# A convolution block and a two-layer state-space block on one core: preparation steps at other places, a smaller share of C on GpSimd, and byte-wise waits of later pools

## The chip, the core and the metric

The program runs on one core of a Trainium2 chip. The time is the device time of one execution, in microseconds; 18147.85 us is the median of three runs. A core has TensorE (PE, matrix products into PSUM), VectorE (DVE), ScalarE (ACT), GpSimd (POOL), and SyncE (SP), whose queue issues most of the transfers. Each engine takes its instructions strictly in the order of its own queue, and waits at an instruction until what it needs is there.

## The reference

Two layers follow one another on x of 32 images, 96 channels, 56 x 56 points, all in float32. Layer 0 is an inverted bottleneck with a depthwise 3 x 3 convolution and a squeeze-and-excite gate; the change doesn't touch it. Layer 1 runs a state-space block (two layers of it) along the 3136 points of each image, then a 1 x 1 fusion and a batch normalisation over everything:

```
h = layernorm(seq);  xs, z = split(h @ in_w)
xc = silu(causal_conv4(xs) + conv_b)
dt, Bm, Cm = split(xc @ xproj_w)            # 6, 16 and 16 columns
delta = softplus(dt @ dt_w + dt_b)
state[t] = exp(delta[t] * A) * state[t-1] + delta[t] * Bm[t] * xc[t]   # 192 x 16 states
y = sum over the 16 of state * Cm + Dp * xc
seq = seq + (y * silu(z)) @ out_w           # twice, then:
out = batchnorm(fus_w @ [seq, relu(gp(mean x))]) + x
```

## The kernel before, in words

**Units and slots.** The change lies in layer 1. A unit is one of the two state-space layers on 784 tokens of one image (four such pieces, LC = 784, make an image): 128 pieces x 2 = 256 units. A unit has 24 slots (`NT`): 192 channels in three groups `k` of 64, 16 states in four groups `j` of 4, two halves `p` of 32 channels. One slot handles 32 channels x 4 states = 128 partitions of 784 tokens.

**What a slot does.** `decay` (L1004, ScalarE) makes exp(delta * A) into `da`, a PSUM tile of which there are two. `inject` (L1041, GpSimd, one for two slots, four slots ahead) makes `bx` = (delta x) * B. `scan` (L1052, VectorE) runs the recurrence over the 784 tokens. The result times C is split by token: the first `LP` tokens by `product` (L1060, VectorE, for two slots at once), for which `bring` (L1029, ScalarE) copies C's first `LP` tokens into PSUM as `cp`, and the remaining tokens by `rest` (L1068, GpSimd). `reduce` (L1099, PE), four slots later, sums the four states into `y`; `gated` (L1110, VectorE) multiplies the finished `y` of a group by silu(z); `seed` (L1086, ScalarE) starts the next group's `y`.

**The first state group goes another way.** For `j` = 0 (slots 0, 1, 8, 9, 16 and 17) it is `fill` (L1018, 32 small matmuls on PE, two records each) that makes (delta x) * B, into a tile of the same two PSUM buffers (`bp`), from delta x transposed (`ut`) and a diagonal matrix of B. There the decay goes to SBUF (`bx` in the profile's rows of L1004). Delta x is transposed by `turn_u(k)` (L848, PE) into a bank and copied by `keep_u(k)` (L854 and L855, ScalarE); B by `turn_b` (L822, PE) and `diagonal` (L831, L832, ScalarE), from where `scatter` writes it to the diagonal of a zeroed DRAM tile `bdiag`, and `fetch` reads it as `diag`.

**Preparation.** While the scans of one unit run, later units are prepared: `center` (L702, PE) and `square` (L707, ScalarE) twice, `variance` (L712, PE), `root` (L719 to L723, ScalarE: add epsilon, log, exp of -1/2, and the three columns that precede the piece), `newton` (L729 to L734, VectorE, three operations that refine the root), `turn` and `normalise` (L744 PE, L751 ScalarE), `turn_back` and `normal` (L757, L761), the causal convolution as four shifted products (L773), `gate` (L789), a block of SiLU with its two table loads (L677, L678), `project_bc` and `store_bc` (L798 PE, L802 ScalarE), `turn_b`, `project_dt` (L810), a block of softplus. All of their products use the two banks of the pool `l1p`; a product waits until the bank that it is given has been read. Before, `root` leaves its result `rs` in columns 16 to 22 of the bank of `var`, where `newton` reads it.

**The order** is written out by hand. Each step has a time in slots, counted in its own unit; its whole part names the slot (modulo 24 for the running unit), its fraction the place in the slot. Steps with a fraction below 0.05 come first in the slot, ahead of the decays of the slot; then come the decays, `bring`, `scan`, `gated`, `product` of the slot before, `rest`, `fill`, the steps from 0.05 to 0.08, `reduce`, and the remaining steps in order of fraction. So `keep_u(1)` at 54.2 stands at the end of slot 6 on ScalarE, `root` at -7.9 at the end of slot 16, `newton` at -6.3 to -6.1 at the end of slot 17, `square` 1 at -9.99 at the start of slot 14.

**Pools.** A pool opened where an earlier one has been closed waits, at its first use, for everything in the memory under it.

Of the kernel before, what the change touches and what calls it, by code (L numbers as in the profile page):

```python
# [11 lines left out]
F32 = mybir.dt.float32  # L12
# [12 lines left out]
NL, NS, DIN, RANK, KC = 2, 16, 192, 6, 4  # L25
LC = 784
HB = LC // 2
LP = 416
NQ = L // LC
RB = HB // W  # L30
DG = 8
# [29 lines left out]
def conv_mamba_kernel(ctx, tc, a, out):  # L61
# [43 lines left out]
    with ExitStack() as ph:  # L105
# [12 lines left out]
        def loadw(name, shape):  # L118
            t = wts.tile(list(shape), F32, name=name, tag=name)
            sp.dma_start(t, a[name])  # L120
            return t
# [406 lines left out]


    with ExitStack() as ph:  # L530
        wts = ph.enter_context(tc.tile_pool(name="l1w", bufs=1))
        dpool = ph.enter_context(tc.tile_pool(name="l1da", bufs=2, space=PSUM))
        cpool = ph.enter_context(tc.tile_pool(name="l1c", bufs=1, space=PSUM))
        ypool = ph.enter_context(tc.tile_pool(name="l1y", bufs=1, space=PSUM))
        pp = ph.enter_context(tc.tile_pool(name="l1p", bufs=2, space=PSUM))
        udram = ph.enter_context(tc.tile_pool(name="l1u", bufs=3, space=DRAM))
        init = ExitStack()
        once = init.enter_context(tc.tile_pool(name="l1i", bufs=1))

        def loadw(name, shape, pool=wts, by=sp):  # L540
            t = pool.tile(list(shape), F32, name=name, tag=name)
            by.dma_start(t, a[name])
            return t
# [27 lines left out]
        outw = wts.tile([128, NL, NB, C], F32, name="outw", tag="outwb")  # L571
        dp = wts.tile([128, NL, NB, 2], F32, name="dp", tag="dpb")
        for to, k, h, src, hc in pieces():
            sp.dma_start(outw[to, :, k, :], a["outw"][src, :, hc, :])
            s.dma_start(dp[to, :, k, :], a["dp"][src, :, hc, KC + 1 : KC + 3])

        araw = loadw("acol", [128, NL, NT], once, s)
        pick = once.tile([128, NS, 2 * DB - DG], F32, name="pick", tag="pick")
        v.memset(pick, 0.0)
        v.tensor_copy(pick[:, :, DB - DG : DB], eye.rearrange("p (s d) -> p s d", s=NS))  # L580
# [48 lines left out]
        for to, k, h, src, hc in pieces():  # L629
            sp.dma_start(wbc[to, :, k, : 2 * NS], a["xpw"][src, :, hc, RANK:])  # L630
            s.dma_start(wbc[to, :, k, 2 * NS : 2 * NS + RANK], a["xpw"][src, :, hc, :RANK])
        for h in range(2):
            for i in range(NL):
                to = wd[h * 64 + 2 * NS : h * 64 + 2 * NS + RANK, i, :, :]
                s.dma_start(to, a["dtw"][:, i, :].rearrange("r (k m) -> r k m", k=NB))
# [13 lines left out]

        xn = wts.tile([C + 1, KC - 1 + LC], F32, name="xn", tag="xn")  # L650
        g.memset(xn[C : C + 1, :], 1.0)
        none = once.tile([TB, TR + 2], F32, name="none", tag="none")
        v.memset(none, 0.0)
        zdram = ph.enter_context(tc.tile_pool(name="l1z", bufs=1, space=DRAM))
        bdiag = [zdram.tile([TB * (TR + 2)], F32, name=f"bdiag{i}", tag=f"bdiag{i}") for i in range(2)]
        for t in bdiag:
            sp.dma_start(t.rearrange("(p r) -> p r", p=TB), none)
        tails = [wts.tile([C + 1, KC - 1], F32, name=f"tail{i}", tag=f"tail{i}") for i in range(NL)]

        init.close()  # L660
        work = ph.enter_context(tc.tile_pool(name="l1", bufs=1))
        MAIN = "natural_log_exp_and_others"
        nch = B * NQ
        TURNS = (range(NK - NK // 2), range(NK - NK // 2, NK))
# [20 lines left out]
        def prepare(n):  # L685
# [14 lines left out]
            def center(h):  # L700
                ps = d["cen", h] = bank(f"cen_{n}_{h}")
                pe.matmul(ps[:C, :HB], cen, seqs[c, i][:, cols(h)], start=True, stop=True)  # L702

            def square(h):
                if h == 0:
                    d["sq"] = wt([128, LC], "sx", 1, n)[:C]
                s.activation(d["sq"][:, cols(h)], d["cen", h][:C, :HB], AF.Square)  # L707
# [7 lines left out]
            def root():  # L715

                va = d["va"] = wt([TK, NK], "va", 1, n)
                rs = d["rs"] = d["var"][:TK, 16 : 16 + NK]
                s.activation(va, d["var"][:TK, :NK], AF.Identity, bias=epsc[:TK])  # L719
                s.activation(rs, va, AF.Ln)  # L720
                s.activation(rs, rs, AF.Exp, scale=-0.5)
                if q > 0:
                    s.copy(xn[:, : KC - 1], tails[i])  # L723
# [121 lines left out]
            def turn_u(k):  # L845
                ps = d["utp", k] = bank(f"ut_{n}_{k}")
                for b in range(4):
                    pe.transpose(ps[: TSZ[b], b * 128 : b * 128 + 128], d["us"][:, k, TOFF[b] : TOFF[b] + TSZ[b]], eye)  # L848
# [17 lines left out]

            steps = [(-20.5, load)]
            for h in range(2):
                steps += [((-11.9, -10.94)[h], lambda h=h: center(h)), ((-10.98, -9.99)[h], lambda h=h: square(h))]
            steps += [(-9.94, variance), (-7.9, root), *[(t, lambda m=m: newton(m)) for m, t in enumerate((-6.3, -6.2, -6.1))]]  # L870
            for m in range(2):
                steps += [((-6.7, -5.5)[m], lambda m=m: turn(m)), (-5.7 + m, lambda m=m: normalise(m))]
                steps += [(-4.5 + m, lambda m=m: turn_back(m)), (-3.9 + m, lambda m=m: normal(m))]
# [4 lines left out]
            for k in range(NB):  # L878
                steps += [(t, lambda k=k, o=o: conv(k, o)) for o, t in taps[k]]
                steps += [((3.1, 5.1, 6.1)[k], lambda k=k: keep("xc", 3, "xs", k))]  # L880
                steps += [((11.06, 11.07, 12.06)[k], lambda k=k: gate(k)), ((12.01, 12.02, 13.01)[k], lambda k=k: keep("z", 3, "zp", k))]
            steps += [(17.6, project_bc), (18.2, store_bc), (18.6, turn_b), (19.2, diagonal)]
            for k in range(NB):
                steps += [((20.6, 21.5, 21.6)[k], lambda k=k: project_dt(k)), ((21.2, 22.1, 22.2)[k], lambda k=k: keep("dl", 1, "dtp", k))]
                steps += [((43.5, 53.6, 56.06)[k], lambda k=k: turn_u(k)), ((44.1, 54.2, 57.01)[k], lambda k=k: keep_u(k))]
            for m in range(6):
                steps += [(26.9 + m, lambda m=m: scatter(*divmod(m, 3)))]
            steps += [(32.1, lambda: spread("delta", d["dl"], slice(0, NB)))]
# [244 lines left out]
        with tc.manual_schedule():  # L1133
            for at in range(min(todo), max(todo) + 1):
                for m in (2, 3):
                    if 0 <= at + m < total and by_pe(at + m) and (at + m) % 2 == 0 and ahead(at + m)[0] == m:
                        lend(at + m)
                if 0 <= at + 4 < total:
                    inject(at + 4)
                for u, step in todo.get(at, ()):  # L1140
                    if u < 0.05:
                        step()
                if 0 <= at - LAG < total:
                    seed(at - LAG)
                if 0 <= at + 1 < total and not by_pe(at + 1):
                    decay(at + 1)
                for x in range(at, at + 5):
                    pair = x // 2 * 2
                    if 0 <= x < total and by_pe(x) and pair - ahead(pair)[x - pair] == at:
                        decay(x)  # L1150
                if 0 <= at < total:
                    bring(at)
                for step in early.get(at, ()):
                    step()
                if 0 <= at < total:
                    scan(at)
                if 0 <= at - LAG - 1 < total:
                    gated(at - LAG - 1)
                if 0 <= at - 1 < total:
                    product(at - 1)  # L1160
                if 0 <= at - 2 < total:
                    save(at - 2)
                if 0 <= at < total:
                    rest(at)
                if 0 <= at + 1 < total and by_pe(at + 1):
                    fill(at + 1)
                for u, step in todo.get(at, ()):
                    if 0.05 <= u < 0.08:
                        step()
                if 0 <= at - LAG < total:  # L1170
                    reduce(at - LAG)
                for u, step in todo.get(at, ()):
                    if u >= 0.08:
                        step()
                for t, tag in BEFORE[at % NT]:
                    fetch(at + t, (tag,))


    with ExitStack() as ph:
        last = ph.enter_context(tc.tile_pool(name="last", bufs=6))  # L1180
        one = ph.enter_context(tc.tile_pool(name="last1", bufs=1))
        mv = one.tile([C, 2], F32, name="mv", tag="mv")
        off = one.tile([C, 1], F32, name="off", tag="off")
        v.tensor_reduce(mv, stats, AX.X, ALU.add)
        v.tensor_scalar(mv, mv, 1.0 / (B * L), None, ALU.mult)
        v.tensor_add(off, mv[:, 0:1], pivot)
        v.tensor_mul(off, off, off)
        v.tensor_sub(mv[:, 1:2], mv[:, 1:2], off)
        inv, sh = bn_fold(one, cp[:, BNG : BNG + 1], cp[:, BNB : BNB + 1], mv[:, 0:1], mv[:, 1:2], C, 1, "bn")
        for b in range(B):  # L1190
            pre = last.tile([C, L], F32, name=f"lp{b}", tag="lp")
            sp.dma_start(pre, pred[b])
            s.activation(pre, pre, AF.Identity, bias=sh, scale=inv)
            g.dma_start(out[b], pre, accum_op=ALU.add, max_dma_last_dim=4 * L // 2)
# [61 lines left out]
```

## Time and profile before

| What | us |
|---|---|
| median of 3 runs (18144.67 to 18149.34) | 18147.85 |
| the profiled execution: its own time | 18136.26 |
| its span (18134.5), layer 0 until | 2901.9 |
| setup of layer 1 and preparation of the first units, until the first scan at | 3023.2 |
| 256 units, until the end of the last scan at | 17836.6 |
| last stage (batch normalisation, residual), until | 18134.5 |

The prediction shows lines of four views. The page's first lines give each engine's busy time, its share of the span and its instructions. A line of the page's groups gives line, engine, operation, what is written from what, the shape, the count, then busy time in us and the mean of one in ns, then the idle time of the engine just ahead of such instructions and what ended most of it. A line of the waits gives engine and line, what it waited for, the total in us, how many times, and the longest. A line of the timeline gives the start in us, the duration, engine, line, operation and shapes, and in brackets the idle time before it and what ended it. The granted clock of PE was 0.919 of full speed on average over the execution: it falls to half for stretches of 3.4 or 6.8 us, at other places in each unit.

### The profile page before, as it was taken

What the parts mean: (1) busy time and instruction counts of PE and PEld (TensorE: products, weight loads), DVE (VectorE), ACT (ScalarE), POOL (GpSimd) and SP (SyncE); (2) the same over time, 40 slices, a digit from 0 to 9 for tenths busy, and PEclk for the clock granted to TensorE, in tenths of its full rate; (3) what the DMA queues carried; (4) which work ended last, traced back from release to release, by engine and by line L of the source; (5) the groups of instructions that cost most, each with busy time, mean ns of one, the idle gap of its engine ahead of it and who ended that gap; (6) DMA issues with size and microseconds to landing.
All of it is one profiled execution on the core that took longest, in us unless ns stands there. A gap on an engine that the chain in (4) does not pass through costs nothing.

```text
span 18134.5 us, 515855 instructions
## 1 busy us (share of the span) xinstructions
PE 15647.2 (86%) x212542; PEld 8205.4 (45%) x212542; DVE 16799.6 (93%) x12755; ACT 14155.9 (78%) x26476; POOL 14150.6 (78%) x6254
## 2 busy tenths in 40 slices
PE   9999998888888888888888888888888888888882
PEld 4444444444444444444444444444444444444441
DVE  9999996999999999999999999999999999999993
ACT  5555555888888888888888888888888888888884
POOL 0000003999999999999999999999999999999993
PEclk9999998999999999999999999999999999999995
DMA  1111113777777777777777777777777777777778
GB/s 35 29 29 29 29 29 93 186 184 187 182 185 182 184 187 184 183 184 183 184 186 184 183 183 182 185 187 184 184 183 183 184 186 184 183 183 183 185 184 219
DMA packets 1723535, 2893.15 MB, mean 160 GB/s; under 512 B 712886, under 2 KB 950670, under 8 KB 1714790
## 3 DMA queue, kind: packets, MB, share of 16 engines
q1 hardware_dynamic: 1712534, 2821.54, 60.4%
q0 software_dynamic: 6656, 38.54, 1.0%
q8 instruction: 1668, 27.33, 0.7%
q14 instruction: 693, 5.68, 0.1%
q10 hardware_dynamic: 1984, 0.07, 0.0%
HBM read 2402.42 MB, written 455.82 MB: 158 GB/s over the span
## 4 chain that ended last, share of the span: by engine, by line
PE 25%; ACT 19%; issue 11%; DMA 10%; DVE 8%; SPq 6%; POOL 4%; ACTq 0%; POOLq 0%; DVEq 0%
PE bp L1018 8%; DVE hh L1052 5%; ACT da L1004 5%; PE y L1099 4%; SPq L982 3%; ACT bx L1004 3%; DVE hc L1060 3%; PE bc L798 3%; PE z L789 3%; DMA deltab<-deltad 3%; PE o L909 2%; DMA bdiag<-bt 2%; SPq L969 2%; POOL hc L1068 2%; POOL bx L1041 2%
## 5 line engine op out<-in xcount | busy, mean ns | idle before, releaser
L1041 POOL TENSOR_TENSOR bx<-ub,B 128x1568 f32<-128x1568 f32 x2304 | 8172.1, 3547 | 16.3 <-DMA diag<-bdiag 13.2
L1052 DVE TENSOR_TENSOR_SCAN hh<-da,state,bx 128x784 f32<-128x784 f32 x3456 | 6273.7, 1838 | 144.8 <-ACT da L1004 133.3
L1068 POOL TENSOR_TENSOR hc<-hh,C 128x736 f32<-128x736 f32 x3072 | 5416.3, 1763 | 714.3 <-DVE hh L1052 398.1
L1004 ACT ACTIVATE da<-deltab,acol 128x784 f32<-128x784 f32 x4608 | 4249.3, 922 | 916.0 <-DVE hh L1052 914.0
L1018 PE MATMUL bp<-diag,ut 91*32 91x91 f32 (+1 forms) x98304 | 3005.8, 280 | 436.3 <-ACT ut L854 351.4
L1099 PE MATMUL y<-hc,rel 128*32 128x392 f32 x24576 | 2911.8, 546 | 522.1 <-ACT y L1086 517.8
L1018 PEld LDWEIGHTS bp<-diag,ut 91*32 91x32 f32 (+1 forms) x98304 | 2652.1, 123 | 1285.3 <-DVE hh L1052 524.1
L1060 DVE TENSOR_TENSOR hc<-hh,cp 128x832 f32<-128x832 f32 x3072 | 3071.8, 1000 | 0.1
L1052 DVE TENSOR_TENSOR_SCAN hh<-bx,state,bp 128x784 f32<-128x784 f32 x1152 | 2117.4, 1838 | 297.8 <-PE bp L1018 269.9
masks.py:197 POOL MEMSET eye<- 128x128 f32 x2 | 0.4, 205 | 2892.6 <-ACT x L427 2892.3
L773 PE MATMUL xs<-xn,wx 97*64 97x392 f32 x12288 | 2240.2, 507 | 0.4 <-ACT xc L784 0.4
L1052 DVE TENSOR_TENSOR_SCAN hh<-da,bx 128x784 f32<-128x784 f32 x1152 | 2025.2, 1778 | 70.6 <-ACT da L1004 65.5
L340 DVE SCALAR_TENSOR_TENSOR h<-hpad,hp,h 128x1568 f32<-128x1568 f32 x1024 | 1895.5, 1851 | 33.2
L1029 ACT COPY cp<-C 128x416 f32<-128x416 f32 x3072 | 1570.4, 511 | 10.3 <-DVE hc L1060 8.8
L1004 ACT ACTIVATE bx<-deltab,acol 128x784 f32<-128x784 f32 x1536 | 1463.4, 953 | 0.0
L773 PEld LDWEIGHTS xs<-xn,wx 97*64 97x64 f32 x12288 | 817.9, 137 | 1366.7 <-issue 1271.0
L1099 PEld LDWEIGHTS y<-hc,rel 128*32 128x32 f32 x24576 | 609.2, 115 | 1521.2 <-ACT y L1086 983.6
L307 PE MATMUL dw<-hpad,diag 32*32 32x392 f32 x36864 | 1111.3, 518 | 0.1
L798 PE MATMUL bc<-xc,wbc 64*64 64x392 f32 x3072 | 634.6, 547 | 318.8 <-DVE rs L734 295.0
L245 PE MATMUL c<-x,w 96*128 96x392 f32 x2048 | 774.2, 520 | 117.8 <-ACT hpad L252 95.8
L864 POOL TENSOR_TENSOR us<-dl,xc 128x392 f32<-128x392 f32 x768 | 788.2, 1026 | 90.4 <-ACT dl L677 90.4
L1052 DVE TENSOR_TENSOR_SCAN hh<-bx,bp 128x784 f32<-128x784 f32 x384 | 682.9, 1779 | 174.3 <-PE bp L1018 138.4
(195 smaller groups left out, 20108.1 us busy)
## 6 DMA issues: line engine op xcount, KB each, us to landing
ub<-ud SPq DMA_DIRECT2D x3072, 196.0 KB
deltab<-deltad SPq DMA_DIRECT2D x3072, 196.0 KB
C<-bcd SPq DMA_DIRECT2D x4096, 98.0 KB
diag<-bdiag SPq DMA_DIRECT2D x1024, 294.8 KB
B<-bcd SPq DMA_DIRECT2D x3072, 98.0 KB
deltad<-dl SPq DMA_DIRECT2D x512, 294.0 KB
ud<-us SPq DMA_DIRECT2D x1536, 98.0 KB
x<-in_x_dram SPq DMA_DIRECT2D x32, 1176.0 KB
```

The lines of the kernel that those rows point to most:

```text
L307: pe.matmul(ps[r][to : to + 32, :HB], diag[src, n, t, :], hb[src, r0 : r0 + RB, dx : dx + W], start=t == 0, stop=t == 8, skip_group_check= ...
L340: v.scalar_tensor_tensor(acc, src, tap, acc, ALU.mult, ALU.add)
L773: pe.matmul(d["xs", k][h * 64 : h * 64 + 64, :HB], wx[:, i, o, k * 64 : k * 64 + 64], xn[:, o + h * HB : o + h * HB + HB], start=o == 0, s ...
L798: pe.matmul(ps[r, :HB], wbc[r, i, k], d["xc"][r, k, :], start=k == 0, stop=k == NB - 1)
L1004: s.activation(das[at], d["delta", k][:, p, :], AF.Exp, scale=acol[:, j, i, 2 * k + p : 2 * k + p + 1])
L1018: pe.matmul(ps[sg * DB : sg * DB + DB, o : o + z], d["ut", k][:z, b, h, p * DB : p * DB + DB], dg[:z, sg // 2, h, x : x + z, sg % 2], star ...
L1029: s.copy(cps[at], data[n]["C", j][:, :LP])
L1041: g.tensor_mul(bx, data[n]["u", k], beside(data[n]["B", j]))
L1052: v.tensor_tensor_scan(hhs[at - p][:, p, :], das.pop(at), bxs.pop(at), state[i][:, t : t + 1] if c % NQ else 0.0, ALU.mult, ALU.add,)
L1060: v.tensor_mul(hcs[at - 1][:, :, :LP], hhs[at - 1][:, :, :LP], beside(cps.pop(at)))
L1068: g.tensor_mul(hcs[at - 1][:, :, LP:], hhs[at - 1][:, :, LP:], beside(data[n]["C", j][:, LP:]))
L1099: pe.matmul(yps[k][r0 : r0 + DB, :HB], rel, hc[:, p, h * HB : h * HB + HB], start=False, stop=j == SG - 1, skip_group_check=True,)
```

## The change

- **Delta x copies.** `keep_u(1)` moves from 54.2 to 54.04, and a new loop, after the decay of the slot and ahead of the decays of the first state group, takes the steps with fractions from 0.03 to 0.05.
- **Squares.** The second `center` moves from -10.94 to -10.97, the second `square` from -9.99 to -10.96, into the new loop of slot 13.
- **Root.** `root` moves from -7.9 to -6.9 (end of slot 17), `newton` from -6.3, -6.2, -6.1 to -5.95, -5.9, -5.85 (slot 18, behind `product`). Its result is a tile `ra` in SBUF instead of columns of the bank of `var`.
- **B's transposes.** `turn_b` moves from 18.6 to 19.15, behind the `reduce` of slot 19.
- **C.** `LP` becomes 424: VectorE and ScalarE take 424 tokens of C, GpSimd 360 instead of 368.
- **Pools.** The later pools get `reuse_waits="tile"`: a tile waits for what lay in its own bytes. The zeros for `bdiag` become a tile of the work pool, set by GpSimd and written from ScalarE's queue; five weight loads of SP and one of ScalarE go to GpSimd's queue, and eight of SP to ScalarE's.

```diff
-LP = 416
+LP = 424
...
-        wts = ph.enter_context(tc.tile_pool(name="l1w", bufs=1))
+        wts = ph.enter_context(tc.tile_pool(name="l1w", bufs=1, reuse_waits="tile"))
...
-        def loadw(name, shape, pool=wts, by=sp):
+        def loadw(name, shape, pool=wts, by=g):
...
-            sp.dma_start(outw[to, :, k, :], a["outw"][src, :, hc, :])
             s.dma_start(dp[to, :, k, :], a["dp"][src, :, hc, KC + 1 : KC + 3])
-        araw = loadw("acol", [128, NL, NT], once, s)
+        araw = loadw("acol", [128, NL, NT], once)
...
             s.dma_start(wbc[to, :, k, 2 * NS : 2 * NS + RANK], a["xpw"][src, :, hc, :RANK])
+            s.dma_start(outw[to, :, k, :], a["outw"][src, :, hc, :])
...
-        none = once.tile([TB, TR + 2], F32, name="none", tag="none")
-        v.memset(none, 0.0)
...
+        init.close()
+        work = ph.enter_context(tc.tile_pool(name="l1", bufs=1, reuse_waits="tile"))
+        none = work.tile([TB, TR], F32, name="none", tag="diag", bufs=1)
+        g.memset(none, 0.0)
         for t in bdiag:
-            sp.dma_start(t.rearrange("(p r) -> p r", p=TB), none)
+            s.dma_start(t[: TB * TR].rearrange("(p r) -> p r", p=TB), none)
-        init.close()
-        work = ph.enter_context(tc.tile_pool(name="l1", bufs=1))
...
-                rs = d["rs"] = d["var"][:TK, 16 : 16 + NK]
+                rs = d["rs"] = wt([TK, NK], "ra", 1, n)
...
-                steps += [((-11.9, -10.94)[h], lambda h=h: center(h)), ((-10.98, -9.99)[h], lambda h=h: square(h))]
-            steps += [(-9.94, variance), (-7.9, root), *[(t, lambda m=m: newton(m)) for m, t in enumerate((-6.3, -6.2, -6.1))]]
+                steps += [((-11.9, -10.97)[h], lambda h=h: center(h)), ((-10.98, -10.96)[h], lambda h=h: square(h))]
+            steps += [(-9.94, variance), (-6.9, root), *[(t, lambda m=m: newton(m)) for m, t in enumerate((-5.95, -5.9, -5.85))]]
...
-            steps += [(17.6, project_bc), (18.2, store_bc), (18.6, turn_b), (19.2, diagonal)]
+            steps += [(17.6, project_bc), (18.2, store_bc), (19.15, turn_b), (19.2, diagonal)]
...
-                steps += [((43.5, 53.6, 56.06)[k], lambda k=k: turn_u(k)), ((44.1, 54.2, 57.01)[k], lambda k=k: keep_u(k))]
+                steps += [((43.5, 53.6, 56.06)[k], lambda k=k: turn_u(k)), ((44.1, 54.04, 57.01)[k], lambda k=k: keep_u(k))]
...
                 for u, step in todo.get(at, ()):
-                    if u < 0.05:
+                    if u < 0.03:
                         step()
                 if 0 <= at - LAG < total:
                     seed(at - LAG)
                 if 0 <= at + 1 < total and not by_pe(at + 1):
                     decay(at + 1)
+                for u, step in todo.get(at, ()):
+                    if 0.03 <= u < 0.05:
+                        step()
```

## The prediction

> **What bounds the kernel now.** I read the page's busy shares first, then its groups, then the table of waits, then one unit of work in the timeline, engine by engine.
>
> ```profile
> span 18134.5 us, 515855 instructions
> PE 15647.2 (86%) x212542; PEld 8205.4 (45%) x212542; DVE 16799.6 (93%) x12755; ACT 14155.9 (78%) x26476; POOL 14150.6 (78%) x6254
> L1041 POOL TENSOR_TENSOR bx<-ub,B 128x1568 f32<-128x1568 f32 x2304 | 8172.1, 3547 | 16.3 <-DMA diag<-bdiag 13.2
> L1052 DVE TENSOR_TENSOR_SCAN hh<-da,state,bx 128x784 f32<-128x784 f32 x3456 | 6273.7, 1838 | 144.8 <-ACT da L1004 133.3
> L1068 POOL TENSOR_TENSOR hc<-hh,C 128x736 f32<-128x736 f32 x3072 | 5416.3, 1763 | 714.3 <-DVE hh L1052 398.1
> L1060 DVE TENSOR_TENSOR hc<-hh,cp 128x832 f32<-128x832 f32 x3072 | 3071.8, 1000 | 0.1
> ```
>
> The four scan groups hold 6144 scans, 24 to a unit, so 256 units. The timeline has the first scan at 3023.2 us and the end of the last at 17836.6: 57.87 us a unit. VectorE stands still before scans for 144.8 + 297.8 + 70.6 + 174.3 = 687.5 us, 2.69 a unit, and is busy otherwise. GpSimd's groups sum to (8172.1 + 5416.3 + 788.2) / 256 = 56.2 us a unit, so GpSimd is within 2 us of being the bound, and its own idle time is mostly waiting for scans. What can be won is VectorE's 2.69 us. The waits say where it goes (columns: total us, times, longest):
>
> ```profile
> DVE hh L1052 <- PE bp L1018: 408.3, 535, 1.7
> POOL hc L1068 <- DVE hh L1052: 398.1, 199, 5.6
> ACT bcs L802 <- PE bc L798: 382.5, 255, 4.9
> PE bp L1018 <- ACT ut L854: 351.4, 256, 1.6
> PE bc L798 <- DVE rs L734: 295.0, 233, 2.7
> DVE hh L1052 <- ACT da L1004: 198.8, 487, 1.2
> ```
>
> 1.59 us a unit is a scan that waits for the 64 matmul records of `fill`, which wait in their turn 1.37 us a unit for ScalarE's copy `ut`. Slots 6 to 8 of the unit at 15229.7 show it:
>
> ```profile
> 15243.89 0.91 ACT L1004 ACTIVATE da<-deltab,acol 128x784 f32<-128x784 f32 x1
> 15244.73 0.94 ACT L1004 ACTIVATE bx<-deltab,acol 128x784 f32<-128x784 f32 x1
> 15245.57 0.47 ACT L784 COPY xc<-xs 128x392 f32<-128x392 f32 x1
> 15245.94 0.26 ACT L854 COPY ut<-ut 120x128 f32<-120x128 f32 x1
> ...
> 15244.04 0.65 PE L848 MATMUL ut<-eye,us 128*120 128x128 f32 x4 [0.20 <-ACT xc L784]
> 15246.25 2.61 PE L1018 MATMUL bp<-diag,ut 120*32 120x120 f32 x64 [1.56 <-ACT ut L854]
> ...
> 15248.99 1.85 DVE L1052 TENSOR_TENSOR_SCAN hh<-bx,state,bp 128x784 f32<-128x784 f32 x1 [1.05 <-PE bp L1018]
> ```
>
> The transposes are done at 15244.69, but ScalarE takes a decay (`bx`) and a copy (`xc`) before it copies them.
>
> **Delta x copies, and what limits the gain.** `keep_u(1)` moves ahead of those two: its first half starts at 15244.73 instead of 15245.94, 1.21 us sooner. Nothing is added; the later `bx` and `xc` have slots to spare. `fill(8)` also needs the buffer of scan 6, which ends at 15241.67 + 3.59 = 15245.26; it starts about 0.13 later (a fill follows its scan so at slot 0), at 15245.39, 0.86 sooner. Its scan stood for 1.05; it now follows scan 7 within about 0.2. The PE work behind it moves up too, so the copy of `ut` in slot 9, which waits 1.61 for PE here, and ScalarE's long run from there to the SiLU block start about 1 us sooner. I take -0.85 us a unit.
>
> **Squares.** The second square goes one decay earlier, so `variance` no longer stands in front of `fill(16)` for 0.99 us (266.7 / 256 = 1.04 a unit in the waits). `fill(16)` is then limited by scan 14's buffer, some 0.2 us sooner than now. Scans 16 and 17 stand for about 0.6 us a unit: -0.15. First centering product, square and copies keep their order.
>
> **Root.** The decay of slot 18 goes ahead of the root's four instructions (0.27 + 0.18 + 0.15 + 0.18, about 0.67 us with their gaps), so scan 18 comes sooner. Newton's three operations move behind product 17, where the root is long done. But `bc` used the bank of `var`, held until Newton's end (the 295.0 above); it now waits only for ScalarE's read of `var`, which comes 0.84 + 0.43 us later than before, behind a decay and a copy. From the SiLU block's end to the start of `bc` it is 15273.25 - 15271.43 = 1.82 us now; then 0.1 + 0.84 + 0.43 + 0.1 + 0.27 + 0.05 = 1.8. So scan 18 gains, and scan 20, which waits for a decay behind `bcs`, gives it back: 0. In one unit of four GpSimd's tiny `xn` memset also falls behind a 3.5 us `bx`; its reader is two slots later.
>
> **B's transposes.** They go behind a reduction (8 matmul records, 0.86 us), so the `bt` copies, for which ScalarE hardly waits today (15278.03), come about 0.8 us late. Decay 21 behind them has 1 us to spare before its scan; the next wait for PE (`ut`, 0.2 us on average) and part of the delay cancel. The reduction itself, and the gate that follows it, come sooner by the same 0.8. Left at scan 22: +0.2. Without the head start of slot 8 it would be +0.45.
>
> **424 tokens.** Product: 16 elements more. Between the 392-wide gate (539 ns) and the 832-wide product (1000 ns) an element costs 461 / 440 = 1.05 ns: +16.8 ns, x 12 = +0.20 a unit. GpSimd: 16 elements fewer at 1763 / 736 = 2.4 ns, x 12 = -0.46, hidden, since it waits for scans. ScalarE's copy: 8 x 12 x about 1 ns = +0.1. VectorE is the limit in about half the unit, elsewhere the 0.2 lies in a wait for ScalarE: +0.1 (both ends: 0 and 0.2).
>
> **Setup and end.** Today the first load of `seq` waits for the zeros of `bdiag`, and centering starts at 2938.14 after 11.12 us idle. Then the load is free of them; but the two zero writes stand on ScalarE's queue before the first square, behind a memset that reuses setup bytes (free at 2927.3). At the rate of GpSimd's 128x384 memset (0.42 us) 3144 columns take 3.4; with two issues the square starts at 2931.7, not 2939.8: -8 (bounds -12 and +3). Six weight loads go to GpSimd's queue (6 x 1.04 by its output rows), eight from SP's to ScalarE's (8 x 0.6): both idle there. SP's steady order is unchanged. The last stage's loads still stand behind the last `pred` store on SP, issued at 17845.4, instead of its landing at 17848.5: -3. Byte-wise waits inside the units change nothing, since these tiles already had their own.
>
> **The port.** Newton's `rs` moves from PSUM to SBUF (`ra`), so its three operations read two SBUF operands. In the row, with one operand in PSUM, they take 0.14 to 0.16 us in the midst of GpSimd's work:
>
> ```profile
> 15270.97 3.54 POOL L1041 TENSOR_TENSOR bx<-ub,B 128x1568 f32<-128x1568 f32 x1
> ...
> 15272.57 0.14 DVE L729 SCALAR_TENSOR_TENSOR nw<-var,va 112x7 f32<-112x7 f32 x1
> 15272.74 0.16 DVE L731 TENSOR_TENSOR nw<-nw,var 112x7 f32<-112x7 f32 x1
> ```
>
> The Trainium skill, "SBUF — State Buffer", section "Who interferes with whom", speaks against the change: a VectorE instruction with two SBUF inputs and a GpSimd instruction that reads SBUF exclude each other for the whole instruction. No row here has that pair, so no run shown confirms it. By the rule the first operation waits out the `bx` under way and the other two, each dependent on the last, a full operation more: 1.76 + 3.55 = 5.3 us, less some 0.5 of slack at `normalise`, less 0.8 of the `bt` wait: +4 a unit, or 1020 us. By the row it is 0. I take the row, because the operations are the same and only 7 elements long, and keep the rule's end for the range.
>
> **Sum.** -0.85 - 0.15 + 0 + 0.2 + 0.1 = -0.70 us x 256 = -179; -8 - 3: -190. The profiled execution took 18136.26 (1.8 around its span); to it that gives 17946. The median of the runs is 11.6 above it, so 17958. I predict **17955**.
>
> **Rivals.**
> - The port, slower: place, slot 18; price up to 4 us a unit, 18147.85 - 190 + 1020 = 18980. It decides from a wait of about 0.7 + 0.4 us a unit, where it eats the gain. One wait alone, the rest of one GpSimd operation (1.3 on average), gives about +0.9 x 256 - 190: 18190. For it: GpSimd has no gap there. Against: the operations are tiny.
> - The head start is used up: `bt` and the product cost and nothing is won because the PE, at a mean clock of 0.919 of full, stretches `fill`. +0.45 + 0.2 less 0.2: +115, 18260. Against: `fill(8)` has 1.37 us of plain waiting.
> - All of VectorE's standing vanishes down to 1.3 us: 18147.85 - 1.3 x 256 - 11 = 17800. Against: ScalarE's SiLU block and `bcs` remain.
> - Byte-wise waits release nothing at setup: 17966; within the likeliest.
>
> **How the numbers follow.** Likeliest, 0.50 (own range 17850 to 18080). All waits gone, 0.08. One wait at the port, 0.15, near zero with both signs (0.04 faster, 0.05 same, 0.06 slower). Full port, 0.20. Head start used up, 0.07, slower. Some 0.02 of the likeliest counts as no change (0.2%, 36 us, is about what a measurement can tell). Faster 0.60, same 0.07, slower 0.33. The range runs from 17800 into the port's case, to 18560 (two of the three waits), leaving out some 0.17 above and 0.03 below.
>
> **What would show it.** Right: the wait of `bp` on `ut` under 0.6 us a unit; VectorE's standing before `bp` under 0.8; scan 18 no longer behind Newton; `bt` copies waiting 0.6 to 0.9 us; Newton at 0.15 us; first square near 2932. Wrong: Newton's operations 1 us or longer or far apart, with `sx_t` waiting for `rs`; or decays standing late at 20 and 22 by more than they gain at 8.

## The result: 6.8% slower, and the profile after

The changed kernel takes 19374.71 us, the median of four runs (19359.51 to 19377.25); the kernel before took 18146.26 beside it (18133.35 to 18149.34). The ratio is 1.0677, with an interval of 1.0658 to 1.0695. I had forecast 17955.

The page of the changed kernel, its first lines and the groups that answer to those of before, with one group that was far too small to be seen there:

```profile
span 19375.5 us, 516086 instructions
PE 15912.1 (82%) x212542; PEld 8240.2 (43%) x212542; DVE 18243.4 (94%) x12754; ACT 14267.3 (74%) x26476; POOL 14121.4 (73%) x6261
...
L1041 POOL TENSOR_TENSOR bx<-ub,B 128x1568 f32<-128x1568 f32 x2304 | 8228.7, 3571 | 17.6 <-DMA diag<-bdiag 13.5
L1068 POOL TENSOR_TENSOR hc<-hh,C 128x720 f32<-128x720 f32 x3072 | 5307.7, 1728 | 1994.1 <-DVE hh L1052 1322.2
L1052 DVE TENSOR_TENSOR_SCAN hh<-da,state,bx 128x784 f32<-128x784 f32 x3456 | 6270.6, 1837 | 86.7 <-ACT da L1004 77.0
...
L1060 DVE TENSOR_TENSOR hc<-hh,cp 128x848 f32<-128x848 f32 x3072 | 3119.7, 1016 | 0.1
...
L729 DVE SCALAR_TENSOR_TENSOR nw<-ra,va 112x7 f32<-112x7 f32 x256 | 1441.9, 5632 | 67.2 <-ACT ra L721 67.2
```

In the groups of VectorE by form, the last one reads before:

```profile
L729 DVE SCALAR_TENSOR_TENSOR nw<-var,va 112x7 f32<-112x7 f32 x256 | 38.3, 150 | 93.3 <-ACT var L721 90.3
```

The span grew by 1241.0 us and VectorE's busy time by 1443.8, while scans, products and GpSimd's groups hardly moved. Nearly all of it is in the last line: Newton's first operation, on 112 x 7 elements, takes 5632 ns in place of 150, and 5632 - 150 = 5.48 us, 256 times, are 1403. GpSimd, which had been within 2 us a unit of the bound, now stands 1322.2 us for scans (398.1 before). VectorE looks busier, but a busy time of 5.6 us for seven elements is a wait that the profile books as work.

The first scan starts at 3018.5 us (3023.2 before) and the last ends at 19080.7, so a unit takes 62.74 us, 4.88 more than before. The table of waits says who stands behind VectorE (total us, times, longest):

```profile
ACT sx_t L751 <- DVE rs L734: 1350.1, 254, 6.1
POOL hc L1068 <- DVE hh L1052: 1322.2, 465, 3.5
PE bt L822 <- ACT sx_t L751: 1199.7, 253, 5.5
...
DVE hh L1052 <- PE bp L1018: 327.7, 352, 13.0
PE bc L798 <- ACT va L719: 310.9, 249, 3.3
ACT bcs L802 <- PE bc L798: 275.1, 255, 3.8
...
DVE hh L1052 <- ACT da L1004: 159.7, 566, 1.1
```

`normalise` (`sx_t`) waits for Newton 5.3 us a unit, and PE's `bt`, behind `normalise` in the order, waits with it. This is what the prediction had named as the sign that it was wrong. The timeline of one unit, with the rows of VectorE and GpSimd alone, shows where the 5.6 us lie:

```profile
15240.48 3.59 POOL L1041 TENSOR_TENSOR bx<-ub,B 128x1568 f32<-128x1568 f32 x1
15240.91 1.85 DVE L1052 TENSOR_TENSOR_SCAN hh<-da,state,bx 128x784 f32<-128x784 f32 x1
15242.68 1.01 DVE L1060 TENSOR_TENSOR hc<-hh,cp 128x848 f32<-128x848 f32 x1
15243.61 5.61 DVE L729 SCALAR_TENSOR_TENSOR nw<-ra,va 112x7 f32<-112x7 f32 x1
15244.01 1.74 POOL L1068 TENSOR_TENSOR hc<-hh,C 128x720 f32<-128x720 f32 x1
15245.69 3.50 POOL L1041 TENSOR_TENSOR bx<-ub,B 128x1568 f32<-128x1568 f32 x1
15249.11 0.12 POOL L737 MEMSET xn<- 97x3 f32 x1
15249.25 0.17 DVE L731 TENSOR_TENSOR nw<-nw,ra 112x7 f32<-112x7 f32 x1
15249.45 0.17 DVE L734 SCALAR_TENSOR_TENSOR rs<-nw,ra 112x7 f32<-112x7 f32 x1
15249.53 1.84 DVE L1052 TENSOR_TENSOR_SCAN hh<-da,state,bx 128x784 f32<-128x784 f32 x1
...
15251.55 1.71 POOL L1068 TENSOR_TENSOR hc<-hh,C 128x720 f32<-128x720 f32 x1 [2.31 <-DVE hh L1052]
```

Newton's first operation starts 0.46 us before the end of the `bx` of 15240.48. It does not get its turn when that ends (15244.07), nor after `rest` (15245.75): it ends at 15249.22, with the second `bx`. GpSimd's next product, the `rest` of slot 19, needs a scan that stands behind Newton on VectorE. So the stall ends just where GpSimd has nothing left that it could do without VectorE. That holds in all of the 253 units in which Newton came while GpSimd was at work: the operation ended together with one of GpSimd's, the third in 242 units and the second in 11, and behind that one GpSimd stood idle, a tiny memset apart, for 2.36 us at the median. The second and third operations then take 0.17 us each, and GpSimd stands until scan 19 is done.

Elsewhere the head start of the delta x copies is there as forecast. Slots 6 to 8, which the prediction showed of before, earlier in the same unit of the changed kernel:

```profile
15213.46 0.91 ACT L1004 ACTIVATE da<-deltab,acol 128x784 f32<-128x784 f32 x1
15214.31 0.26 ACT L854 COPY ut<-ut 120x128 f32<-120x128 f32 x1
...
15214.84 0.97 ACT L1004 ACTIVATE bx<-deltab,acol 128x784 f32<-128x784 f32 x1
...
15214.99 1.69 PE L1018 MATMUL bp<-diag,ut 120*32 120x120 f32 x64 [0.73 <-ACT ut L855]
...
15217.46 1.82 DVE L1052 TENSOR_TENSOR_SCAN hh<-bx,state,bp 128x784 f32<-128x784 f32 x1
```

The copy of `ut` now stands ahead of the decay `bx`, `fill(8)` is done at 15216.68, and scan 8 follows scan 7 without the 1.05 us of standing. On average over the units VectorE stood 0.94 us ahead of that scan before, and stands 0.01 now.

### The profile page after: what moved, and what is told of

Read it like the earlier page. It is cut to its first block, busy times and chain, and to the rows that moved or that the text cites. A ratio compares the mean times of both kernels' runs of the same rounds, so it can differ in the third digit from the quotient of the medians.

```text
span 19375.5 us, 516086 instructions
## 1 busy us (share of the span) xinstructions
PE 15912.1 (82%) x212542; PEld 8240.2 (43%) x212542; DVE 18243.4 (94%) x12754; ACT 14267.3 (74%) x26476; POOL 14121.4 (73%) x6261
## 4 chain that ended last, share of the span: by engine, by line
PE 31%; ACT 20%; issue 17%; DVE 15%; DMA 7%; POOL 5%; SPq 4%; ACTq 0%; DVEq 0%; POOLq 0%
PE dw L307 5%; DVE hc L1060 5%; DVE nw L729 4%; PE dt L810 4%; DVE hh L1052 4%; ACT da L1004 4%; PE c L419 4%; PE bp L1018 3%; PE y L1099 3%; PE c L245 3%; ACT bx L1004 2%; POOL hc L1068 2%; DMA bcd<-bcs 2%; ACT sx_t L751 2%; POOL bx L1041 2%
## 5 line engine op out<-in xcount | busy, mean ns | idle before, releaser
L1068 POOL TENSOR_TENSOR hc<-hh,C 128x720 f32<-128x720 f32 x3072 | 5307.7, 1728 | 1994.1 <-DVE hh L1052 1322.2
L1018 PE MATMUL bp<-diag,ut 91*32 91x91 f32 (+1 forms) x98304 | 2825.4, 269 | 476.5 <-DVE hh L1052 413.5
L1060 DVE TENSOR_TENSOR hc<-hh,cp 128x848 f32<-128x848 f32 x3072 | 3119.7, 1016 | 0.1
L1018 PEld LDWEIGHTS bp<-diag,ut 91*32 91x32 f32 (+1 forms) x98304 | 2531.7, 118 | 1273.1 <-DVE hh L1052 719.8
L1029 ACT COPY cp<-C 128x424 f32<-128x424 f32 x3072 | 1575.5, 513 | 12.0 <-DVE hc L1060 6.4
L729 DVE SCALAR_TENSOR_TENSOR nw<-ra,va 112x7 f32<-112x7 f32 x256 | 1441.9, 5632 | 67.2 <-ACT ra L721 67.2
L751 ACT ACTIVATE sx_t<-ct,rs 112x96 f32<-112x96 f32 x1792 | 471.2, 343 | 1350.1 <-DVE rs L734 1350.1
L822 PE MATMUL bt<-bsel,bcs 128*91 128x8 f32 (+1 forms) x2048 | 379.0, 314 | 1200.0 <-ACT sx_t L751 1199.7
L822 PEld LDWEIGHTS bt<-bsel,bcs 128*91 128x91 f32 (+1 forms) x2048 | 354.9, 280 | 1380.7 <-ACT sx_t L751 1380.1
```

What stands on the lines that cost most here:

```text
L729: v.scalar_tensor_tensor(d["nw"], rs, -0.5, va, ALU.mult, ALU.mult)
L1018: pe.matmul(ps[sg * DB : sg * DB + DB, o : o + z], d["ut", k][:z, b, h, p * DB : p * DB + DB], dg[:z, sg // 2, h, x : x + z, sg % 2], star ...
L1029: s.copy(cps[at], data[n]["C", j][:, :LP])
L1060: v.tensor_mul(hcs[at - 1][:, :, :LP], hhs[at - 1][:, :, :LP], beside(cps.pop(at)))
L1068: g.tensor_mul(hcs[at - 1][:, :, LP:], hhs[at - 1][:, :, LP:], beside(data[n]["C", j][:, LP:]))
```

## The experiments

Two theories stood against each other. *Operands*: what is slow is Newton with all its operands in SBUF, and it waits for GpSimd. *Order*: the new places of root, Newton and B's transposes are what is slow, and the long L729 is a symptom. Within the first it was open how long the wait lasts: for the operation under way, or until GpSimd runs dry. All ratios are to the kernel before, run on the same chip.

**1. The same order, but the root's result in PSUM.** Seven columns of the y bank are free in these slots, so nothing moves and no bank is held. (The first three units, prepared before there is such a bank, use the bank of `var`.)

```diff
-                rs = d["rs"] = wt([TK, NK], "ra", 1, n)
+                rs = d["rs"] = yps[1][:TK, 400 : 400 + NK] if 1 in yps else d["var"][:TK, 16 : 16 + NK]
```

> The changed kernel with one line undone in kind: the root's result lies in PSUM again, in seven free columns of the y bank, so that the bank of var stays free and every step stays where the change put it. Operand theory (a VectorE instruction with two SBUF operands waits for GpSimd): Newton's three operations back to 0.15-0.17 us each, the unit at 56.3 to 57.2 us, total 17,750 to 17,970. Order theory (the new places of root, Newton and B's transposes make it slow): still 19,200 to 19,400.

Measured: 17954.15 us, ratio 0.9884 (0.9870 to 0.9899). One line takes 1.0677 - 0.9884 = 7.9%, some 1440 us, away. The groups of this run, by form:

```profile
L731 DVE TENSOR_TENSOR nw<-nw,y 112x7 f32<-112x7 f32 x253 | 41.0, 162 | 8.8
L734 DVE SCALAR_TENSOR_TENSOR rs<-nw,y 112x7 f32<-112x7 f32 x253 | 40.8, 161 | 8.7
L729 DVE SCALAR_TENSOR_TENSOR nw<-y,va 112x7 f32<-112x7 f32 x253 | 39.9, 158 | 0.0
```

The same three operations at the same place take 0.16 us each. The order theory falls; and the whole of the change but this line is worth 1.2%, close to what the prediction's sum said.

**2. The kernel before, with only the root's result in SBUF.**

```diff
-                rs = d["rs"] = d["var"][:TK, 16 : 16 + NK]
+                rs = d["rs"] = wt([TK, NK], "ra", 1, n)
```

> The kernel before with only the root's result in SBUF (ra), all places as before. Order theory: 18,150, or a few us less since the bank of var is free sooner. One-operation theory (Newton's first operation waits for the GpSimd operation under way): it arrives at 42.6 us of the unit, bx ends at 44.8, so 2.2 us, about +460: 18,600. Run-dry theory (it waits until GpSimd has nothing left that is ready, which is the end of bx(22) at 49.96): 7.3 us, less at most 0.5 of standing that it covers, +6.8 to 7.3 x 256: 19,880 to 20,020.

Measured: 19639.08 us, ratio 1.0817 (1.0799 to 1.0835). One line is enough to make the kernel before slower than the changed one. Its first operation:

```profile
L729 DVE SCALAR_TENSOR_TENSOR nw<-ra,va 112x7 f32<-112x7 f32 x256 | 1527.0, 5965 | 84.7 <-ACT ra L721 82.9
```

The three operations together take 5965 + 402 + 667 ns = 7.03 us a unit, 6.6 more than before, where the run-dry theory had 7.3. The time is some 240 us, 0.94 a unit, short of that theory's range. The larger part is that shorter stall (the last section shows the units in which the wait is broken up); the rest is that it covers more standing than the 0.5 us that I had allowed: VectorE's waits ahead of scans 18, 20 and 22, 0.67 us a unit before, are gone in this run.

**3. The changed kernel without Newton.**

```diff
-                    v.scalar_tensor_tensor(d["nw"], rs, -0.5, va, ALU.mult, ALU.mult)
...
-                    v.tensor_mul(d["nw"], d["nw"], rs)
...
-                    v.scalar_tensor_tensor(to, d["nw"], 1.5, rs, ALU.add, ALU.mult)
```

> The changed kernel without Newton's three operations (the refinement of the root is left out; the root goes to normalise as it is). Operand theory: the stall goes with them, 17,700 to 17,950. Order theory: the decay ahead of the root and turn_b behind the reduction are still there, so it stays above 19,000.

Measured: 17939.25 us, ratio 0.9882 (0.9867 to 0.9897), the same as experiment 1. With one operand in PSUM, Newton costs nothing that can be measured.

**4. Root and Newton wholly as before, the rest of the change kept.**

```diff
-                rs = d["rs"] = wt([TK, NK], "ra", 1, n)
+                rs = d["rs"] = d["var"][:TK, 16 : 16 + NK]
...
-            steps += [(-9.94, variance), (-6.9, root), *[(t, lambda m=m: newton(m)) for m, t in enumerate((-5.95, -5.9, -5.85))]]
+            steps += [(-9.94, variance), (-7.9, root), *[(t, lambda m=m: newton(m)) for m, t in enumerate((-6.3, -6.2, -6.1))]]
```

> The changed kernel with root, Newton and the root's PSUM columns all as before; delta x copies, squares, B's transposes, 424 tokens and pools as changed. Operand theory: 17,800 to 17,970, since the root's part of the sum was 0. Against the run with the root at the new place but in PSUM it says what the move itself is worth: 0 by the prediction, within 30 us.

Measured: 17879.48 us, ratio 0.9847 (0.9832 to 0.9862). The move of the root alone, which I had put at 0, costs 0.0037 x 18147.85 = 67 us, give or take 38: at its new place Newton stands between scans 18 and 19, and VectorE stands 0.45 us ahead of scan 20 for its decay (0.10 in this run).

**5. Which operation waits.** In the changed kernel `va` goes to the y bank instead, and `ra` stays in SBUF. Newton's first operation then has an operand in PSUM, and the others have not.

```diff
-                va = d["va"] = wt([TK, NK], "va", 1, n)
+                va = d["va"] = yps[1][:TK, 400 : 400 + NK] if 1 in yps else wt([TK, NK], "va", 1, n)
```

> The changed kernel with va instead of the root's result in the free columns of the y bank (ra stays in SBUF). Newton's first operation then reads one SBUF and one PSUM operand, the second and third still two in SBUF. If it is decided operand by operand: L729 back to 0.15-0.17 us, and L731 takes the wait in its place, from about 44.5 to the end of bx(22) at 49.9, 5.4 us, total 19,200 to 19,400. If it is the first VectorE operation after ScalarE's root that waits (for the result in SBUF to be seen), L729 still takes 5 us or more.

Measured: 19254.62 us, ratio 1.0612 (1.0591 to 1.0633). The groups by form:

```profile
L731 DVE TENSOR_TENSOR nw<-nw,ra 112x7 f32<-112x7 f32 x256 | 1397.4, 5458 | 8.9
L734 DVE SCALAR_TENSOR_TENSOR rs<-nw,ra 112x7 f32<-112x7 f32 x256 | 42.5, 166 | 8.8
L729 DVE SCALAR_TENSOR_TENSOR nw<-ra,y 112x7 f32<-112x7 f32 x253 | 39.0, 154 | 0.0
```

The wait has gone over to L731, with nearly its whole length. So it is decided for each instruction by where its operands lie, and has nothing to do with ScalarE's result being seen late.

**6. The wait by itself.** Idle operations in the kernel before, on constants, with no one before or behind them but the engine's own order.

```diff
+        idle = wts.tile([128, 16], F32, name="idle", tag="idle")
...
+            def dummy(two):
+
+                if two:
+                    v.tensor_mul(idle[:TK, :NK], eye[:TK, :NK], eye[:TK, 64 : 64 + NK])
+                else:
+                    v.tensor_copy(idle[:TK, NK : 2 * NK], eye[:TK, :NK])
...
-            steps = [(-20.5, load)]
+            steps = [(-20.5, load), (3.8, lambda: dummy(False)), (3.9, lambda: dummy(True)), (20.9, lambda: dummy(True))]
```

> The kernel before with three idle VectorE operations of 112x7 in each unit, on constants: at the end of slot 3 a copy with one SBUF operand and then a product of two SBUF operands, at the end of slot 20 the same product. Nothing depends on them and they depend on nothing, so what they take is their wait for GpSimd. One-operation theory: the copy 0.1 us, the product in slot 3 waits from 8.9 to the end of bx at 11.57, 2.7 us; in slot 20, from 51.40 to the end of rest at 51.67, 0.3 us; total +3.1 x 256: 18,940. Run-dry theory: in slot 3 GpSimd can go on through bx and rest(3) to 13.29 and then needs scan 5, so 4.4 us; in slot 20 the same 0.3, since GpSimd then waits for scan 21; total +4.7 x 256: 19,350. If the two SBUF operands alone made it slow, whatever GpSimd does, slot 20 would take as long as slot 3.

Measured: 19534.56 us, ratio 1.0761 (1.0740 to 1.0783); the 185 us above the run-dry theory's figure are a longer standing ahead of scan 8, 1.64 us a unit against 0.94 before. First slot 3 of a unit, then the end of slot 20:

```profile
15263.67 3.53 POOL L1049 TENSOR_TENSOR bx<-ub,B 128x1568 f32<-128x1568 f32 x1
15264.46 4.45 DVE L873 COPY idle<-eye 112x7 f32<-112x7 f32 x1
15267.14 1.75 POOL L1076 TENSOR_TENSOR hc<-hh,C 128x736 f32<-128x736 f32 x1
15268.83 0.15 DVE L871 TENSOR_TENSOR idle<-eye 112x7 f32<-112x7 f32 x1
...
15310.07 1.77 POOL L1076 TENSOR_TENSOR hc<-hh,C 128x736 f32<-128x736 f32 x1
15310.39 1.47 DVE L871 TENSOR_TENSOR idle<-eye 112x7 f32<-112x7 f32 x1
```

The group of the copy:

```profile
L873 DVE COPY idle<-eye 112x7 f32<-112x7 f32 x256 | 1118.3, 4369 | 0.0
```

The length came as the run-dry theory had it: 4.45 us, through the `bx` and through the `rest` behind it. In slot 20, where GpSimd has one product under way and then needs scan 21, the wait is what is left of that product, and 0.16 us when there is none under way; in 24 of 254 units, where a `bx` was just ending, it waited through the product behind it too. But it was the copy that waited in slot 3, although it has one SBUF operand; the product behind it found GpSimd at rest. I had taken the copy for a control, and it is none: the run doesn't show that it takes two SBUF inputs to wait. What all the operations that waited have in common is that every operand lies in SBUF; those with one in PSUM went through at 0.14 to 0.17 us.

**7. Delta x copies alone**, in the kernel before.

```diff
-                steps += [((43.5, 53.6, 56.06)[k], lambda k=k: turn_u(k)), ((44.1, 54.2, 57.01)[k], lambda k=k: keep_u(k))]
+                steps += [((43.5, 53.6, 56.06)[k], lambda k=k: turn_u(k)), ((44.1, 54.04, 57.01)[k], lambda k=k: keep_u(k))]
...
-                    if u < 0.05:
+                    if u < 0.03:
...
+                for u, step in todo.get(at, ()):
+                    if 0.03 <= u < 0.05:
+                        step()
```

> The kernel before with the head start of keep_u(1) alone. The prediction's term: -0.85 us a unit, 217 us: 17,930, the wait of bp on ut under 0.6 a unit. Rival (the head start is used up by the PE's clock and slot 10): 18,050 or more.

Measured: 17885.79 us, ratio 0.9849 (0.9834 to 0.9864), 274 us less. In its table of waits PE's 351.4 us for `bp` behind the first copy, L854, have shrunk to the second line here:

```profile
PE bp L1018 <- ACT ut L855: 29.6, 41, 0.7
PE bp L1018 <- ACT ut L854: 22.7, 64, 0.4
```

**8. B's transposes alone**, in the kernel before: `turn_b` at 19.15 instead of 18.6.

> The kernel before with turn_b alone moved behind the reduction of slot 19. The prediction's term without the head start: +0.45 us a unit, +115 us: 18,265; the bt copies wait 0.6 to 0.9 us. Rival: the decay behind them hides it and the reduction that comes sooner pays it back, 18,130 to 18,180.

Measured: 18382.47 us, ratio 1.0132 (1.0116 to 1.0149), 240 us more, twice the term. The copies of `bt` wait as expected, and the decays behind them are late:

```profile
DVE hh L1052 <- PE bp L1018: 556.0, 693, 13.7
...
DVE hh L1052 <- ACT da L1004: 273.6, 581, 1.3
ACT bt L831 <- PE bt L822: 181.3, 255, 2.2
DVE hh L1052 <- POOL bx L1041: 84.3, 61, 1.7
```

181.3 / 256 = 0.71 us a unit for `bt`; VectorE then stands 0.27 us longer ahead of scan 21, 0.28 ahead of scan 8, and 0.39 ahead of the next unit's scan 0, a place that I had not looked at. Ahead of scan 8 it is `fill(8)` that takes longer, 2.66 us against 2.38, at a granted clock of 0.61 against 0.73 (means over the units).

**9. B's transposes back, with 424 tokens**, on top of experiment 4: `turn_b` at 18.6 again.

> Root and Newton as before, turn_b at its old place, but 424 tokens: with the two runs that had neither and both of these last two undone, it splits their joint cost. By the prediction's terms (turn_b +0.2, tokens +0.1 us a unit) it stands 26 us above the one with 416 tokens and 51 below the one with both: 17,770 to 17,830. If the tokens cost what VectorE pays for them in each product, 0.2 us a unit: 51 above, 17,795. If turn_b costs what it did alone (some 0.9 us a unit), it is within 20 us of the one with 416.

Measured: 17828.52 us, ratio 0.9827 (0.9811 to 0.9844).

**10. And 416 tokens too.** `LP = 416`, on top of experiment 9.

> Root and Newton as before, as in the run before this one that had that, and now also turn_b at its old place and 416 tokens: head start, squares and pools remain of the change. By the prediction's terms these two cost +0.2 and +0.1 us a unit, so it is 77 us faster than with them: 17,800. If they are hidden it stays at 17,870 to 17,890.

Measured: 17743.03 us, ratio 0.9773 (0.9758 to 0.9787), the fastest of all and 2.3% faster than before. It keeps the head start, the squares, and the pools and setup. Between 9 and 10 the tokens cost 98 us, give or take 40; in the profiles a unit is 0.22 us longer with 424, of which VectorE's twelve products, each 16 ns longer, make 0.19. Against experiment 4 the two steps together are worth 136 us, where the prediction's terms had 77. In the fastest run GpSimd's groups make up the whole unit (8253.0 + 5415.2 us in the two large ones, against an idle time of 268.6 ahead of `rest`), so both engines are full.

## Why the prediction was wrong, step by step

The runs stand on each other, so the whole difference falls into terms (difference of two ratios x 18147.85, each good to about 40 us; 0.0677 x 18147.85 = 1229 is their sum but for rounding):

| Step | predicted | measured | from |
|---|---|---|---|
| delta x copies | -217 | -274 | experiment 7 |
| squares, setup and end | -49 | -138 | 10 against 7 |
| 424 tokens | +26 | +98 | 9 against 10 |
| B's transposes, with the head start | +51 | +36 | 4 against 9 |
| root's new place | 0 | +67 | 1 against 4 |
| Newton's operands in SBUF | 0 | +1439 | result against 1 |
| sum | -190 | +1228 | |

- **The step that failed is the port**, and in it the sentences "By the row it is 0. I take the row, because the operations are the same and only 7 elements long". The row was no near row: it had an operand in PSUM, and that is just what the change takes away. Length doesn't come into it, since what is paid is GpSimd's work, not Newton's. What the change would have brought without this term is what experiment 1 measured, 17954.15. That the forecast, 17955, agrees within 1 us is luck: the other terms were off by -57, -89, +72, -15 and +67 us, which nearly cancel.
- **The rival "The port, slower" had the right mechanism**, and its price, +4 us a unit, was too small. Its 5.3 us of waiting are near the 5.5 measured, but come about in another way: it made the first operation wait out one `bx` and the others one operation each, and its sum, 1.76 + 3.55, holds only two of these three waits; in fact the first waits for what is left of one operation and through two more, and the others not at all. And nothing came off it. I had taken 1.3 us off for slack at `normalise` and for `bt`; instead of that, VectorE stands 1.15 us ahead of the next scan 0, where `fill` comes late behind the stalled preparation (1.96 us after the end of scan 22, 0.21 before).
- The Trainium skill ("SBUF — State Buffer", section "Who interferes with whom") says that a VectorE instruction with two SBUF inputs and a GpSimd instruction that reads SBUF exclude each other, and that copies in a two-port mode do so too. The runs agree for two inputs, 5632 ns against 150, and the copy's 4369 ns fit, though no run shows in which mode it ran. They add that one wait can last for all the work that GpSimd has ready, which a price of one operation misses.
- **Delta x copies**: right, and undersized. VectorE stood 0.94 us ahead of scan 8 before and 0.21 with the copies alone; the rest of the 274 us lies elsewhere in the unit. Part of it is a thing that the prediction had not looked at: `fill(8)` does not only start 0.75 us sooner after scan 6, it also takes 1.87 us in place of 2.38, and the granted clock over it is 0.92 on average, not 0.73. One rival had feared the opposite. Why the clock falls less often there was not tried. (Of the 468 stretches at half the clock before, 387 last 3.4 or 6.8 us, and 74 last 10.2.)
- **Squares**: right in sign. VectorE's standing ahead of scans 16 and 17 goes from 0.88 us in experiment 7 to 0.44 in experiment 10, three times the 0.15 that I had given it, and the unit from 56.88 to 56.38, 126 us in all. The two runs also differ in pools, so these are not shown to be the squares' alone.
- **424 tokens**: the working, 16.8 ns a product and +0.20 a unit, was right. The half that I took was not: VectorE pays it in every pair of slots. The rest of the 98 us, some 45, is about the uncertainty of the term.
- **B's transposes**: with the head start +36, which fits the predicted +51 but, give or take 40, hardly differs from nothing; without it, twice the predicted +0.45 a unit.
- **Root**: not 0, and the "0" had been a gain and a loss that I set equal.
- **Setup**: the forecast, 8 us sooner, was right in sign and somewhat small. The first squares start at 2940.0, not near 2932, but layer 0, which the change doesn't touch, ended at 2912.1 in this execution and at 2901.9 in that of before. Counted from there the squares come 27.9 us later instead of 37.9, and the first scan 106.4 instead of 121.3. Over all profiles the squares come after 37.9 to 38.6 us with the old setup and 27.8 to 28.3 with the new. Layer 0 ended at 2901.3 to 2913.0 in the five profiles with the old setup and at 2910.1 to 2916.9 in the seven with the new; whether the moved loads have a part in that was not tried. The last stage takes 269.4 us from the end of the last scan (273.6 before), where 3 less were forecast.

## What to carry to other kernels

Look at where the operands of every VectorE instruction lie, not only at its size: beside a full GpSimd, one without a PSUM operand can cost as much as GpSimd has ready, and here seven free columns of a PSUM bank were worth 1440 us. When a change moves an operand from PSUM to SBUF, a duration of before is no price for the new form. And an instruction whose busy time is far beyond its size is a wait; put the other engines' timeline beside it.

## What had not been expected

The wait doesn't end with the GpSimd operation under way, and yet it is not always to the end. In experiment 2 Newton arrives right behind scan 17, which is also what GpSimd's `rest(17)` waits for. In 211 of 253 units the first operation waited until GpSimd ran dry, 7.2 us at the median. In 38 it went through at the end of `bx(20)`, and then the second and third, with one exception, waited for one operation each; in two it came when none was under way, and in two it went through part of the way. One of the 38, again with the rows of VectorE and GpSimd alone:

```profile
5113.26 3.56 POOL L1041 TENSOR_TENSOR bx<-ub,B 128x1568 f32<-128x1568 f32 x1
5114.69 1.85 DVE L1052 TENSOR_TENSOR_SCAN hh<-bx,state,bp 128x784 f32<-128x784 f32 x1 [0.40 <-PE bp L1018]
5116.45 0.39 DVE L729 SCALAR_TENSOR_TENSOR nw<-ra,va 112x7 f32<-112x7 f32 x1
5116.76 1.76 POOL L1068 TENSOR_TENSOR hc<-hh,C 128x736 f32<-128x736 f32 x1
5116.88 1.66 DVE L731 TENSOR_TENSOR nw<-nw,ra 112x7 f32<-112x7 f32 x1
5118.46 3.50 POOL L1041 TENSOR_TENSOR bx<-ub,B 128x1568 f32<-128x1568 f32 x1
5118.58 3.41 DVE L734 SCALAR_TENSOR_TENSOR rs<-nw,ra 112x7 f32<-112x7 f32 x1
```

In all of the 38, scan 17 had ended 0.11 to 0.29 us before the end of that `bx`; in the 204 that waited to the end with a `bx` under way it had ended 0.30 us before or earlier. In experiment 5, where scan 17 ends more than a microsecond before, operations that arrive 0.25 us before the end of `bx` wait all the same. So it seems to matter whether GpSimd's next operation was ready 0.3 us before the one under way ends: if so it goes ahead of VectorE, and so does the one behind it. That is argued from the times, and two units do not fit well: with scan 17 ended 0.31 us before, the operation went through behind the product that followed, and with 1.56 us at the end of the `bx` itself. No run sets this margin on purpose, and how GpSimd comes to hold its place was not tried.
